# First tree's masks made by TensorE and ScalarE, three rows' statistics moved, experts' second product by halves, last tile stored in quarters

## The chip, the cores and the metric

The kernel runs on one core of one Trainium2 chip. A core has TensorE (PE in the profile, with its weight loads listed as PEld), VectorE (DVE), ScalarE (ACT), GpSimd (POOL) and SyncE (SP), which here only issues transfers. The metric is the device time of one execution in microseconds (us), as the median of several runs; lower is better.

## The reference

The input `x` is 4 rows of 512 tokens by 128 features. Six residual steps follow, each on the layer norm of `x`:

```python
x = x + 0.5 * fff_attention(ln(x))     # T: three trees q, k, v, then attention
x = x + attention(ln(x))               # h: 16 heads, rope, causal
x = x + 0.5 * fff_attention(ln(x))     # t
x = x + 0.5 * experts(ln(x))           # e: 8 experts, top 2, and a shared one
x = x + mamba(ln(x))                   # s: a scan over time, 16 states
x = x + 0.5 * experts(ln(x))           # f
```

A tree has 15 nodes and 16 leaves. Each token walks down four levels by the signs of the node scores and ends in one leaf; the output is that leaf's small network (128 to 64 to 128):

```python
sel = one_hot(leaf, 16)
hidden = relu(einsum('nd,ldh->lnh', x, w1) + b1) * sel.T[:, :, None]
out = einsum('lnh,lho->no', hidden, w2) + sel @ b2
```

An expert computes `(silu(x @ w1.T) * (x @ w3.T)) @ w2.T`, weighted by its gate.

## The kernel before

Everything is written as small generators, one for each row (0 to 3) and step, and `TIMES` gives each a planned start and end. The main loop always advances the job whose next step is planned earliest, so the code of many rows and steps is interleaved into one program text. From that text the framework makes the queue of each engine when the program is built: it may take an instruction ahead of older ones of the same engine if its inputs are expected to be ready. Waits between engines are semaphores, and each engine works through its own queue in order. SP's queue holds nearly all transfers, also in order.

**A tree step.** `tree_prep` computes the layer norm (`stats`: `bn_stats` at L290, `bn_aggr` at L292, an inverse root by tiny VectorE instructions from L300 to L283, the shift at L308; `layer_norm` at L316 or L318), turns it (`features`, L324 to L333), scores the nodes in three matmuls (`mm3`, L173 to L175: a product in two rounded parts), makes bits of the signs (L356) and multiplies by the leaf paths (L359). An entry of that product is zero where the token is in that leaf. `taken` (L361) is this as bytes for 48 leaves; it is written to memory (L363), and six transfers (L369) read it back, so that each leaf's row of 512 bytes lies on 64 partitions. That is `mask`, eight chunks of 128 hidden units by 512 tokens for each of the three trees, in two buffers. `sel` (L375) is the same selection in a float format for the bias product (L413).

`tree_main` then takes 24 chunks: `first` makes the hidden layer of a chunk (three matmuls into a PSUM bank of role `tree_mm`, or `start` for every other of the first eight) and applies bias and mask in one VectorE instruction, `full` (L400). `second` multiplies by the second weights into `tree_acc` (L410), five chunks later. For row 0 the weights come from the caller's arrays and are split into two parts by ScalarE and GpSimd or VectorE (`split_tree`, L161 and L162); they are also kept in memory for the other rows. `second_bias` folds a bias in (L234 to L240). Buffers of role `stage` (five) hold what is to be split, buffers of role `ring` (seven) hold weights. PSUM has eight banks; `tree_tr` is the role of the small products.

The calls 1 to 3 of `tree_prep` are those of rows 1, 3 and 2 in their first tree step. Each begins with `stats`, which reads only the loaded `x`, so the framework was free to put those instructions early.

**An expert step.** `expert_main` makes two hidden tiles for each expert (`u0`, `u1`, at L765 to L772) and multiplies them by the second weights in `second` (L780): for each of four 128-token tiles of the row, first the half with `u0`, then the half with `u1`, into one PSUM bank. ScalarE scales the result by the gate (L790) and GpSimd adds it to `x` (L791). The shared expert, which comes last, is added by VectorE in one instruction (L793). After the last step `store` writes the row out (L1013).

Of the kernel before, what the change touches and what calls it, by code (L numbers as in the profile page):

```python
# [15 lines left out]
F32 = mybir.dt.float32  # L16
F32R = mybir.dt.float32r
# [4 lines left out]
ALU = mybir.AluOpType  # L22
AX = mybir.AxisListType

P = 128
B, S, D = 4, 512, 128
NT = S // P
EPS = 1e-5

LEAVES, LEAF_W, DEPTH = 16, 64, 4  # L30
NODES = LEAVES - 1
NCH = LEAVES * LEAF_W // P
# [47 lines left out]
EXPERTS, INTER = 8, 256  # L80
# [32 lines left out]
def macaron(ctx: ExitStack, tc: tile.TileContext, t: dict, stages: int = 6):  # L113
    nc = tc.nc
# [6 lines left out]
    def bank(role):  # L121
        return psum.tile([P, S], F32, tag=role, name=role, bufs=BANKS[role])
# [4 lines left out]
    def tiny(shape, tag, bufs=2):  # L127

        n = int(np.prod(shape[1:]))
        if tag not in turns:  # L130
            first = taken_of[0]
            taken_of[0] += bufs * n
            assert taken_of[0] <= SCRATCH
            turns[tag] = cycle([scratch[:, first + n * i : first + n * i + n] for i in range(bufs)])
        out = next(turns[tag])
        if len(shape) == 2:
            return out
        names = "abcd"[: len(shape) - 1]
        sizes = dict(zip(names, shape[1:]))
        return out.rearrange(f"p ({' '.join(names)}) -> p {' '.join(names)}", **sizes)  # L140

    def work(role, shape=(S,), dtype=F32):

        return wp.tile([P, *shape], dtype, tag=role, name=role, bufs=BUFS[role])
# [11 lines left out]
    def flat(a):  # L156
        return a if len(a.shape) == 2 else a.rearrange("p a b -> p (a b)")
# [31 lines left out]
    x = [rows[:, b] for b in range(B)]  # L189
# [12 lines left out]
    leafpath, ident_h, future_t = (whole[:, ts(k, P)] for k in range(3))  # L202
    future = whole[:, 3 * P :]


    at = {}
    col = 0
# [59 lines left out]
    def inverse_root(out, v, s):  # L267

        shape = list(out.shape)
        y = tiny(shape, f"root_{shape[1]}", 4)  # L270
        nc.vector.tensor_scalar(
            y.bitcast(I32), v.bitcast(I32), -0.5, float(0x5F3759DF), ALU.mult, ALU.add
        )

        h = tiny(shape, f"square_{shape[1]}", 4)
        nc.vector.tensor_mul(s, y, v)
        nc.vector.tensor_mul(h, s, y)
        nc.vector.scalar_tensor_tensor(s, h, -10.0 / 3, h, ALU.add, ALU.mult)
        nc.vector.scalar_tensor_tensor(y, s, 5.0, y, ALU.add, ALU.mult)
        a = 0.375  # L280
        nc.vector.scalar_tensor_tensor(s, y, -0.5 * a**3, v, ALU.mult, ALU.mult)
        nc.vector.tensor_mul(s, s, y)
        nc.vector.scalar_tensor_tensor(out, s, 1.5 * a, y, ALU.add, ALU.mult)  # L283

    def stats(b, role, square=False):

        st = tiny([P, NT, 6], "bn", 4)
        mv = tiny([P, NT, 2], "mv", 4)
        for i in range(NT):
            nc.vector.bn_stats(st[:, i, :], x[b][:, i, :])  # L290
        for i in range(NT):
            nc.vector.bn_aggr(mv[:, i, :], st[:, i, :])  # L292
        n = 2 if square else 1
        rstd, shift = (tiny([P, n, NT], f"{r}_{n}", 4) for r in ("rstd", "shift"))

        ps = bank(role)
        var, step = (
            ps[:, k * n * NT : (k + 1) * n * NT].rearrange("p (n t) -> p n t", n=n) for k in range(2)
        )
        nc.vector.tensor_scalar_add(var[:, 0, :], mv[:, :, 1], EPS)  # L300
        if square:

            nc.vector.scalar_tensor_tensor(
                var[:, 1, :], var[:, 0, :], EPS, mv[:, :, 1], ALU.mult, ALU.add
            )
        inverse_root(rstd, var, step)
        mean = mv[:, :, 0].unsqueeze(1).to_broadcast([P, n, NT])
        nc.vector.scalar_tensor_tensor(shift, mean, -1.0, rstd, ALU.mult, ALU.mult)  # L308
        return [(rstd[:, k, :], shift[:, k, :]) for k in range(n)]

    def layer_norm(b, rstd, shift, on_act=False, role="ln"):
        ln = work(role)
        for i in range(NT):
            out, by, to = ln[:, ts(i, P)], rstd[:, i : i + 1], shift[:, i : i + 1]
            if on_act:
                nc.scalar.activation(out, x[b][:, i, :], AF.Identity, scale=by, bias=to)  # L316
            else:
                nc.gpsimd.tensor_scalar(out, x[b][:, i, :], by, to, ALU.mult, ALU.add)  # L318
        return ln
# [25 lines left out]
        return tuple(w), second_weights(k)  # L345

    def tree_prep(b, st):
        ln = layer_norm(b, *stats(b, "tree_tr")[0], st.call == 0)
        yield
        st.xn = xn = features(ln, "tree_tr")  # L350
        yield

        ps = bank("tree_tr")
        mm3(ps, nodes, xn)
        bits = work("bits", dtype=BF16)
        nc.vector.tensor_scalar(bits, ps, at["node_b"], 0.0, ALU.add, ALU.is_ge)  # L356
        yield
        ps = bank("tree_tr")
        nc.tensor.matmul(ps, lhsT=leafpath, rhs=bits, start=True, stop=True)  # L359
        taken = work("taken", dtype=U8)[:ALL_LEAVES]  # L360
        nc.vector.tensor_scalar(taken, ps[:ALL_LEAVES], 0.0, None, ALU.is_equal)  # L361
        rows = t["fff_taken"][st.call]
        nc.sync.dma_start(out=rows, in_=taken)  # L363
        st.masks = []
        for k in range(TREES):
            mask = work("mask", (NCH, S), U8)
            pairs = rows[k * LEAVES : (k + 1) * LEAVES].rearrange("(c l) s -> l c s", l=2)
            for m in range(2):
                nc.sync.dma_start(  # L369
                    out=mask[m * LEAF_W : (m + 1) * LEAF_W],  # L370
                    in_=pairs[m : m + 1].to_broadcast([LEAF_W, NCH, S]),
                )
            st.masks.append(mask)
        st.sel = work("sel", dtype=F32R)
        nc.vector.tensor_scalar(st.sel, ps, 0.0, None, ALU.is_equal)  # L375

    def tree_main(b, st):
        xn = st.xn
# [376 lines left out]
    def expert_main(b, st, last):  # L755
        xn = st.xn
        weights = [fetch_expert(e) for e in range(AHEAD)]

        def first(e, c):
            w13 = [weights[e][0][:, k, :] for k in range(2)]  # L760
            ps1, ps3 = bank("moe_1"), bank("moe_3")
            mm3(ps1, [m[:, ts(c, P)] for m in w13], xn)
            mm3(ps3, [m[:, ts(2 + c, P)] for m in w13], xn)
            u = work(f"u{c}")
            nc.scalar.activation(u, ps1, AF.Tanh, scale=0.5)  # L765
            nc.vector.scalar_tensor_tensor(u, u, 1.0, ps1, ALU.add, ALU.mult)  # L766
            if (2 * e + c) % POOL_E[0] < POOL_E[1]:
                v = work("v3")
                nc.scalar.copy(v, ps3)
                nc.gpsimd.tensor_mul(u, u, v)  # L770
            else:
                nc.vector.tensor_mul(u, u, ps3)  # L772
            return u

        def second(e, h):
            w2 = weights[e - e % 4][1]
            acc = bank("moe_acc")
            for i in range(NT):
                for c in range(2):
                    nc.tensor.matmul(  # L780
                        acc[:, ts(i, P)],
                        lhsT=h[c][:, ts(i, P)],
                        rhs=w2[:, e % 4 * 2 + c, :],
                        start=(c == 0),
                        stop=(c == 1),
                    )
            if e < EXPERTS:
                y = work("y")
                for i in range(NT):
                    nc.scalar.mul(y[:, ts(i, P)], acc[:, ts(i, P)], st.comb[:, i, e : e + 1])  # L790
                nc.gpsimd.tensor_add(flat(x[b]), flat(x[b]), y)  # L791
            else:
                nc.vector.scalar_tensor_tensor(  # L793
                    flat(x[b]), acc, 0.25, flat(x[b]), ALU.mult, ALU.add
                )

        later = Later(LAG_EXPERT)
        for e in range(EXPERTS + 1):
            if e + AHEAD < EXPERTS + 1:
                weights.append(fetch_expert(e + AHEAD))  # L800
            h = []
            for c in range(2):
                h.append(first(e, c))
                later.step()
                yield
            later.add(partial(second, e, h))
        while later.queue:
            later.step()
            if later.queue:
                yield  # L810
        if last:
            store(b)


# [370 lines left out]
def _constants():  # L1185

    f = np.float32
# [46 lines left out]
    for q in range(GROUPS):  # L1234
# [10 lines left out]
        "lower": np.broadcast_to(lower, (P, EXPERTS, EXPERTS)),  # L1245
        "state_w": np.concatenate([np.zeros((P, 6, P), f), gather.reshape(P, 1, P)], axis=1),
        "spread": spread.reshape(P, GROUPS * P),
    }, head


# [99 lines left out]
```

## Time and profile before

| What | Value |
|---|---|
| Median of the runs | 1130.06 us (1129.55 to 1131.53, three runs) |
| Profiled execution, its own time | 1134.71 us |
| Span of that execution | 1132.9 us |
| First product with masked values (L410) | begins 27.24 us after the start |
| First product of the k tree in row 0 | begins 34.18 us after the start |
| Last product of the last row | ends about 1128.3 us |
| Transfers of 512-byte mask rows (L369) | 48, 256 KB each |

The profiled execution is one run, 4.65 us slower than the median; of its 1134.71 us 1132.9 are the span in which the instructions of the profile lie. All times inside an execution are counted from the start of that span. Each line of a timeline is an engine, a line of the code, the operation, what it writes and reads, and the idle time ahead of it with what ended it.

### The profile page before, as it was taken

The page shows a single profiled execution, that of the slowest core. Times are in us where ns is not written, and L with a number is a line of the kernel's source. Part 1 is how long each engine was busy: PE and PEld are TensorE (multiplying, and loading weights), DVE is VectorE, ACT ScalarE, POOL GpSimd, SP SyncE. Part 2 cuts the span into 40 slices and gives each one's busy share as a digit, 9 for nine tenths or more (in the row PEclk, how much of TensorE's full clock was granted, in tenths as well). Part 3 has the DMA queues.
Part 4 walks back from the last instruction along what each step waited for, and adds up shares of the span by engine and source line. Part 5 has one row for each costly group of instructions (what it writes and reads, how often), then busy time and mean ns, then how long its engine had stood idle before and what let it go on. Part 6 is the DMA issues. An engine that isn't in the chain of part 4 may idle for free.

```text
span 1132.9 us, 16461 instructions
## 1 busy us (share of the span) xinstructions
PE 1065.0 (94%) x5536; PEld 717.4 (63%) x5536; DVE 903.5 (80%) x2151; ACT 516.4 (46%) x1078; POOL 408.3 (36%) x392
## 2 busy tenths in 40 slices
PE   3999999999999999999999999999598989997998
PEld 2666655566666767765566766567276646754787
DVE  4566886587576887775799997899989989999864
ACT  2231423332322555444443544465576557564544
POOL 2215231002100323220324651356626647666523
PEclk9999999999999999999999999999899989997999
DMA  7885845321542212243743334832137424742320
GB/s 217 261 254 168 284 109 119 84 69 57 123 124 93 65 37 69 87 112 115 208 137 139 117 94 107 277 130 107 38 117 254 133 66 146 249 121 70 113 88 10
DMA packets 79651, 146.41 MB, mean 129 GB/s; under 512 B 7536, under 2 KB 39664, under 8 KB 79568
## 3 DMA queue, kind: packets, MB, share of 16 engines
q1 hardware_dynamic: 79280, 145.07, 42.6%
q8 instruction: 44, 0.72, 0.3%
q14 instruction: 39, 0.32, 0.1%
q10 hardware_dynamic: 288, 0.30, 0.1%
HBM read 125.35 MB, written 13.70 MB: 123 GB/s over the span
## 4 chain that ended last, share of the span: by engine, by line
PE 61%; DVE 17%; issue 4%; ACT 4%; POOL 2%; DMA 1%; SPq 1%; POOLq 0%; ACTq 0%; DVEq 0%
PE tree_acc L410 9%; PE moe_acc L780 7%; DVE states L990 6%; PE head_acc L608 4%; PE head_sc L640 4%; PE moe L173 4%; PE head_max L564 4%; PE moe L175 3%; PE moe L174 3%; DVE states L989 3%; PE tree_mm L173 3%; PE tree_mm L175 3%; PE tree_mm L174 3%; PE state_acc L941 2%; DVE u L766 2%
## 5 line engine op out<-in xcount | busy, mean ns | idle before, releaser
L991 POOL TENSOR_TENSOR states<-states,cs 128x512 f32<-128x512 f32 x128 | 163.8, 1284 | 146.0 <-DVE states L990 87.8
L410 PE MATMUL tree_acc<-full,ring 128*128 128x512 f32 x384 | 193.4, 599 | 5.9 <-DVE full L400 4.9
L572 DVE CUSTOM_DVE_ANT_0 head_max<-head_max,kept 128x128 f32<-128x128 f32 (+3 forms) x256 | 126.8, 495 | 61.0 <-PE head_max L564 58.5
L400 DVE SCALAR_TENSOR_TENSOR full<-tree_mm,kept,mask 128x512 f32<-128x512 f32 x188 | 137.8, 746 | 42.4 <-PE tree_mm L175 37.7
L656 ACT ACTIVATE pt<-head_sc 128x512 f32<-128x512 f32 (+1 forms) x176 | 95.3, 559 | 139.2 <-PE head_sc L648 132.4
L780 PEld LDWEIGHTS moe_acc<-ring,u 128*128 128x128 f32 x1152 | 141.9, 195 | 21.2 <-DVE u L772 6.2
L990 DVE TENSOR_TENSOR_SCAN states<-decay,states 128x512 f32<-128x512 f32 x128 | 154.8, 1216 | 0.5 <-ACT decay L988 0.2
L780 PE MATMUL moe_acc<-ring,u 128*128 128x128 f32 x1152 | 146.4, 280 | 5.3 <-DVE u L772 3.1
L173 PE MATMUL moe<-xl,ring 128*128 128x512 f32 x288 | 129.1, 448 | 13.3 <-DVE u L766 4.7
L791 POOL TENSOR_TENSOR kept<-kept,y 128x512 f32<-128x512 f32 x64 | 83.0, 1298 | 142.2 <-ACT y L790 133.7
L988 ACT ACTIVATE decay<-dts,kept 128x512 f32<-128x512 f32 x128 | 88.5, 696 | 83.9 <-DVE states L990 67.0
L765 ACT ACTIVATE u<-moe 128x512 f32<-128x512 f32 x144 | 86.4, 601 | 72.2 <-PE moe L175 70.5
L174 PE MATMUL moe<-xh,ring 128*128 128x512 f32 x288 | 116.8, 405 | 0.0
L175 PE MATMUL moe<-xh,ring 128*128 128x512 f32 x288 | 115.7, 402 | 0.0
L766 DVE SCALAR_TENSOR_TENSOR u<-u,moe 128x512 f32<-128x512 f32 x144 | 97.4, 678 | 17.7 <-ACT u L765 15.2
L790 ACT ACTIVATE y<-moe_acc,scratch 128x128 f32<-128x128 f32 x256 | 73.3, 367 | 74.5 <-PE moe_acc L780 72.6
L548 POOL TENSOR_SCALAR km<-k_bias,kept 128x512 fp32r<-128x512 f32 x64 | 43.6, 699 | 157.2 <-PE head_sc L640 110.6
L173 PE MATMUL tree_mm<-xl,ring 128*128 128x512 f32 x188 | 98.1, 524 | 0.2 <-DVE states L990 0.2
L173 PEld LDWEIGHTS moe<-xl,ring 128*128 128x128 f32 x288 | 55.1, 191 | 63.5 <-DVE u L766 13.5
L410 PEld LDWEIGHTS tree_acc<-full,ring 128*128 128x128 f32 x384 | 70.8, 191 | 38.4 <-issue 19.9
L564 PE MATMUL head_max<-km,q_bias 120*128 120x512 f32 (+2 forms) x192 | 92.0, 479 | 1.1 <-ACT p L446 1.1
L989 DVE TENSOR_TENSOR states<-state_b,dtxs 128x512 f32<-128x512 f32 x128 | 85.9, 683 | 4.7 <-DMA dtxs<-state_rows 3.6
(257 smaller groups left out, 1946.1 us busy)
## 6 DMA issues: line engine op xcount, KB each, us to landing
ring<-moe_parts SPq DMA_DIRECT2D x72, 512.0 KB
ring<-tree_parts SPq DMA_DIRECT2D x42, 512.0 KB
ring<-in_fff_w SPq DMA_DIRECT2D x24, 512.0 KB
mask<-fff_taken SPq DMA_DIRECT2D x48, 256.0 KB
ring<-in_moe_w SPq DMA_DIRECT2D x16, 512.0 KB
dts<-state_rows SPq DMA_DIRECT2D x32, 256.0 KB
dtxs<-state_rows SPq DMA_DIRECT2D x32, 256.0 KB
moe_parts<-moe_w SPq DMA_DIRECT2D x9, 512.0 KB
```

Of the source, the lines that this page charges most:

```text
L173: nc.tensor.matmul(ps, lhsT=lh, rhs=rl, start=start, stop=False)
L174: nc.tensor.matmul(ps, lhsT=ll, rhs=rh, start=False, stop=False)
L175: nc.tensor.matmul(ps, lhsT=lh, rhs=rh, start=False, stop=stop)
L400: nc.vector.scalar_tensor_tensor(full, ps, neg_b1[:, n : n + 1], st.masks[k][:, c, :], ALU.max, ALU.mult)
L410: nc.tensor.matmul(acc, lhsT=weights[k][1][:, c, :], rhs=h, start=(c == 0), stop=False)
L564: nc.tensor.matmul(view, lhsT=qs[:R_MAX, g, ts(i, P)], rhs=km[j0 // 2][:R_MAX, j0 % 2 : j0 % 2 + each, :kw], start=True, stop=True,)
L572: nc.vector.tensor_tensor_reduce(view[:, n, :], view[:, n, :], future[:, S - kw :], -1.0, float(np.finfo(np.float32).max), ALU.add, ALU.mi ...
L766: nc.vector.scalar_tensor_tensor(u, u, 1.0, ps1, ALU.add, ALU.mult)
L780: nc.tensor.matmul(acc[:, ts(i, P)], lhsT=h[c][:, ts(i, P)], rhs=w2[:, e % 4 * 2 + c, :], start=(c == 0), stop=(c == 1),)
L989: nc.vector.tensor_mul(h, bs, dtx[g])
L990: nc.vector.tensor_tensor_scan(h, dA, h, 0.0, ALU.mult, ALU.add)
L991: last = nc.gpsimd.tensor_mul(h, h, cs[:, q])
```

## The change

There are four edits.

1. In the first call of `tree_prep` (row 0), the masks of the q tree no longer go through memory. A new constant `leaf_rows` (16 leaves by 8 chunks of 128, one where the hidden unit belongs to the leaf) is loaded on ScalarE's queue into a `stage` buffer and copied into a second one in the rounded format. `sel` is made ahead of `taken`. Then eight matmuls with 16 contraction rows spread `sel` over the 128 hidden units of each chunk, and eight ScalarE copies turn them into bytes. The k and v masks of row 0, and all masks of later calls, come by transfer as before.
2. In calls 1, 2 and 3 the first `bn_stats` may not be taken ahead of what VectorE was given before it in the program text.
3. `second` of the experts goes through all four tiles with `u0` and then through all four with `u1`; the flags that open and close the accumulation are set once for the bank.
4. For the shared expert of the last row in the last step, products keep the order by tile, the addition to `x` is made in four instructions, and each quarter is stored by a transfer of its own.

```diff
+    raw_rows, leaf_rows = (work("stage", [NCH * P], dt)[:LEAVES] for dt in (F32, F32R))
+    nc.scalar.dma_start(out=raw_rows, in_=t["leaf_rows"])
+    nc.scalar.copy(leaf_rows, raw_rows)
...
-            nc.vector.bn_stats(st[:, i, :], x[b][:, i, :])
+            first = nc.vector.bn_stats(st[:, i, :], x[b][:, i, :])
+            if late and i == 0:
+                tc.keep_in_program_order(first)
...
-        ln = layer_norm(b, *stats(b, "tree_tr")[0], st.call == 0)
+        ln = layer_norm(b, *stats(b, "tree_tr", late=0 < st.call < B)[0], st.call == 0)
...
+        st.sel = work("sel", dtype=F32R)
+        if st.call == 0:
+            nc.vector.tensor_scalar(st.sel, ps, 0.0, None, ALU.is_equal)
         taken = work("taken", dtype=U8)[:ALL_LEAVES]
...
+            st.masks.append(mask)
+            if st.call == 0 and k == 0:
+
+                for c in range(NCH):
+                    ps_c = bank("tree_tr")
+                    nc.tensor.matmul(
+                        ps_c, lhsT=leaf_rows[:, ts(c, P)], rhs=st.sel[:LEAVES], start=True, stop=True
+                    )
+                    nc.scalar.copy(mask[:, c, :], ps_c)
+                continue
...
-        st.sel = work("sel", dtype=F32R)
-        nc.vector.tensor_scalar(st.sel, ps, 0.0, None, ALU.is_equal)
+        if st.call:
+            nc.vector.tensor_scalar(st.sel, ps, 0.0, None, ALU.is_equal)
...
-            for i in range(NT):
-                for c in range(2):
...
+            at_end = last and b == B - 1 and e == EXPERTS
+            order = [(c, i) for c in range(2) for i in range(NT)]
+            for c, i in sorted(order, key=lambda ci: ci[::-1]) if at_end else order:
+                nc.tensor.matmul(
+                    acc[:, ts(i, P)],
+                    lhsT=h[c][:, ts(i, P)],
+                    rhs=w2[:, e % 4 * 2 + c, :],
+                    start=(c == 0 and (at_end or i == 0)),
+                    stop=(c == 1 and (at_end or i == NT - 1)),
+                )
...
-            else:
+            elif not at_end:
...
+            else:
+                for i in range(NT):
+                    out = x[b][:, i, :]
+                    nc.vector.scalar_tensor_tensor(out, acc[:, ts(i, P)], 0.25, out, ALU.mult, ALU.add)
+                    nc.sync.dma_start(out=t["out"][b, ts(i, P)], in_=out)
...
-        if last:
+        if last and b < B - 1:
             store(b)
...
+        "leaf_rows": np.kron(np.eye(LEAVES, dtype=f), np.ones((1, LEAF_W), f)),
```

More of the change, by code (lines that the diff above doesn't have):

```diff
@@ L283, in inverse_root, with stats @@
         nc.vector.scalar_tensor_tensor(out, s, 1.5 * a, y, ALU.add, ALU.mult)
-    def stats(b, role, square=False):
+    def stats(b, role, square=False, late=False):
         st = tiny([P, NT, 6], "bn", 4)
@@ L372, in tree_prep @@
                 )
-            st.masks.append(mask)
-        st.sel = work("sel", dtype=F32R)
-        nc.vector.tensor_scalar(st.sel, ps, 0.0, None, ALU.is_equal)
+        if st.call:
+            nc.vector.tensor_scalar(st.sel, ps, 0.0, None, ALU.is_equal)
     def tree_main(b, st):
@@ L777, in second @@
             acc = bank("moe_acc")
-            for i in range(NT):
-                for c in range(2):
[L780 to L786, printed above, removed]
+            at_end = last and b == B - 1 and e == EXPERTS
[8 more added lines that the diff above has]
+                )
             if e < EXPERTS:
```

## The prediction

> **What bounds the kernel now.** I read the page first: its busy table, its slices, its chain of work.
>
> ```profile
> PE 1065.0 (94%) x5536; PEld 717.4 (63%) x5536; DVE 903.5 (80%) x2151; ACT 516.4 (46%) x1078; POOL 408.3 (36%) x392
> ...
> PE   3999999999999999999999999999598989997998
> ...
> PE 61%; DVE 17%; issue 4%; ACT 4%; POOL 2%; DMA 1%; SPq 1%; POOLq 0%; ACTq 0%; DVEq 0%
> ```
>
> TensorE is busy in nearly every slice of 28 us. Only the first (3 tenths) and those from 800 us on, where VectorE's scan limits, have holes. In stretches of 5 us PE is at 5.00 nearly throughout from 30 to 580 us; so what is won ahead of 30 us should move all that follows, if the queues keep their order. The front is therefore read next, in order of time, VectorE and ScalarE first:
>
> ```profile
> 7.04 0.17 DVE L282 TENSOR_TENSOR tree_tr<-tree_tr,scratch 128x4 f32<-128x4 f32 x1
> ...
> 8.59 0.29 DVE L290 BATCH_NORM_STATS2 scratch<-kept 128x6 f32<-128x128 f32 x1 [1.38 <-DMA kept<-in_x]
> 8.80 0.14 DVE L283 SCALAR_TENSOR_TENSOR scratch<-tree_tr,scratch 128x4 f32<-128x4 f32 x1
> 8.86 1.22 DVE L162 TENSOR_TENSOR ring<-stage,ring 128x1024 fp32r<-128x1024 f32 x1
> 9.99 0.15 DVE L308 SCALAR_TENSOR_TENSOR scratch<-scratch 128x4 f32<-128x4 f32 x1
> ...
> 10.18 1.65 ACT L316 ACTIVATE ln<-kept,scratch 128x128 f32<-128x128 f32 x4 [1.40 <-DMA ring<-in_fff_w]
> ```
>
> Row 0's last step of the root (L283) stands behind row 1's first statistics, which wait 1.38 us for row 1's `x`; then a weight split comes between it and L308, and the layer norm starts at 10.18. The same timeline further on:
>
> ```profile
> 17.55 0.68 DVE L361 TENSOR_SCALAR taken<-tree_tr 48x512 uint8<-48x512 f32 x1 [1.36 <-PE tree_tr L359]
> ...
> 19.94 1.37 SPq L369 DMA_DIRECT2D mask<-fff_taken  x2
> ...
> 21.41 0.57 SPq L166 DMA_DIRECT2D stage<-in_fff_w  x1
> ...
> 26.44 0.75 DVE L400 SCALAR_TENSOR_TENSOR full<-tree_mm,kept,mask 128x512 f32<-128x512 f32 x1 [2.94 <-DMA mask<-fff_taken]
> ...
> 27.24 2.08 PE L410 MATMUL tree_acc<-full,ring 128*128 128x512 f32 x2 [4.92 <-DVE full L400]
> ...
> 28.78 1.05 ACT L161 CAST ring<-stage 128x1024 fp32r<-128x1024 f32 x1 [5.80 <-DMA stage<-in_fff_w]
> ```
>
> The selection is known at 18.2, but the q masks land at 26.4; PE has filled its banks and stands 4.92 us. In 27.24 to 30.39 the table by stretches grants PE a clock of 0.50. The k weights, issued behind the masks on SP, land at 28.8. And the end:
>
> ```profile
> 1128.99 0.69 DVE L793 SCALAR_TENSOR_TENSOR kept<-moe_acc,kept 128x512 f32<-128x512 f32 x1 [2.60 <-POOL kept L791]
> 1129.71 0.39 SPq L1013 DMA_DIRECT2D out<-kept  x1
> ```
>
> The last addition waits for GpSimd's addition of the expert before (ends 1128.96), not for PE (done at 1128.3).
>
> **The parts, and their cost.** Savings are minus.
>
> (a) *Row 0's layer norm.* Without row 1's statistics ahead of it, L283 can follow L282 at 7.24 and L308 at 7.45. ScalarE then decides: its weight cast runs 7.74 to 8.78, so the layer norm starts at 8.8 behind it (-1.4) or at 7.6 ahead of it (-2.6); if the split still stands before L308, at 10.2 (0). The load of `leaf_rows` (64 KB, some 0.2 us at the 280 to 370 GB/s of 3 to 9 us) may delay that cast by 0.2. Its issue (0.45, as the two ScalarE issues before it) and its copy of 1024 columns (1.05, as the cast of 1024 columns at L161) fall in ScalarE's idle 1.37 and 2.55 us ahead of 4.96 and 7.74; without that cover the copy would cost its 1.05. I take -1.4 + 0.2 = -1.2, the order that the queue has now; bounds -2.6 to +1.3 (0 + 0.2 + 1.05).
>
> (b) *PE's stall for the masks.* After (a), `sel` is ready at 17.55 - 1.2 + 0.7 = 17.05 (now first, at `taken`'s place). One matmul (0.4) and one ScalarE copy of 512 columns (0.58, the row of L332) later the first chunk is there at about 18.1, and `full` can run 8 us sooner. ScalarE is idle from 15.7 to 22.7 (6.98 us before L239), enough for 8 x 0.58 = 4.6. Six banks hold waiting chunks, so the copies may have only one or two of the eight; with one, a chunk takes matmul, copy and two handovers, about 1.2, still under the 1.55 us in which PE does a chunk (period of 36.66 and 38.21). So the 4.92 go, and the slow clock with them: 27.24 to 30.39 held 3.15 us of what takes 1.55 later, 1.6. Sum -6.5; bounds -6.5 to -4.9.
>
> (c) *Eight more matmuls on PE*, 512 columns each: 0.23 start to start where PE runs at its later pace, 0.42 in the first 17 us. +1.8; bounds +1.8 to +3.4.
>
> (d) *Is the k tree ready?* In the trace its weights are whole at 32.3 (cast 28.78, GpSimd's part to 32.3) and PE comes to them at 34.18; it would now come at 34.18 - 1.2 - 6.5 + 1.8 = 28.3. Two mask issues (1.37) leave SP ahead of the load, and `taken` comes 1.2 - 0.7 = 0.5 earlier, so it is issued near 19.5. If it takes the 7.4 us it took (21.41 to 28.78, beside 512 KB of mask rows that are now gone), then 1.05 and 2.38, it is whole at 30.4: +2.1. If it moves like the last store (0.5 us until data flow, 256 KB from 1130.6 to 1131.8), 512 KB land 3.3 after issue, the weights are whole at 26.3, and it costs nothing. If it comes no sooner at all, +4.0. The first mask rows were what it shared the transfers with, so I lean to the short end: +0.5. The k masks, issued behind it, are needed at about 29.5 and have 9 us where they had 13.
>
> (e) *Statistics moved.* Row 1's took 0.85 + 0.37 + about 2.0 us of VectorE that was idle; rows 2 and 3 had 1.2 us each early, and their tiny steps already came later. Row 1's now stand behind its tenth chunk, near 30; its layer norm comes near 35, and its transposes, at 45.74 before, are wanted near 39.5: 4 us of slack. VectorE is busy 2.0 to 3.4 of 5 us from 35 to 65, so PE's three chunk banks bridge it. Rows 2 and 3 fall in 95 to 130, where VectorE has 2.8 to 4.8 of 5. +0.3; bounds 0 to +2.4 (all of the two rows' instructions in PE's way).
>
> (f) *Experts' products by halves.* The work is the same. PE waits for the second half where the first could run, 0.97 us of matmuls. The view of waits:
>
> ```profile
> PE moe_acc L780 <- DVE u L772: 3.1, 6, 0.7
> ```
>
> 3.1 us in six waits is the most to win, and some of it lies where the scan limits. -1.0; bounds -3.1 to 0.
>
> (g) *End by quarters.* The additions still start at 1128.99. The first quarter (0.35, row of L468) is issued at 1129.4, and four issues of 0.39 end at 1130.9, 0.8 later than the one did. The one transfer moved data from 1130.6 to 1131.8, of which a quarter needs 0.3 instead of 1.2. So +0.8 - 0.9 = -0.1; bounds -0.5 to +0.8. The Trainium skill, in DMA: Bandwidth & Descriptors (Rules for kernel authors), advises to merge small transfers, since under 64 KB most of the time is overhead; by the section Anatomy of one DMA, with about 2.0 us fixed each, the last of four would land at 1132.9, which speaks against this part and would make it +1.1 instead of -0.1 against the 1131.8 of the trace.
>
> Sum: -1.2 - 6.5 + 1.8 + 0.5 + 0.3 - 1.0 - 0.1 = **-6.2 us**. The profiled execution's 1134.71 would be 1128.5 (span 1126.7); the median 1130.06 becomes **1123.9**.
>
> **The rivals.**
>
> *A, the transfers hide it.* From 22 to 48 us the transfers' mean share is about 1.0, and the k weights come no sooner than 32.3. Then PE only gains its 1.9 us of lateness there: -1.9 + 0.3 - 1.0 - 0.1, 1127.4. For it: that share. Against it: from 17 to 22 the share is 0.0 to 0.4, and in 30 to 130 PE waits for no transfer.
>
> *B, a new wait in ScalarE's queue: slower.* The cast of the k weights stands ahead of some mask copies in ScalarE's queue. All behind it then waits until the weights land. If they land at 25.0, copies resume at 26.05 and `full` at 26.7 (0.3 later than in the trace), and the eight matmuls come on top: +2.1. If they land at 28.8 as now, it is +4.0 + 1.8. Midway, +4.0, with (e), (f) and (g) at -0.8: +3.2, 1133.2. It decides if the cast precedes the copies and the weights land after 23. For it: ScalarE waited 5.80 us on this load already. Against it: the copies can run from 17.5 on, long before.
>
> *C, another order later.* Queues are not in the order of the code (row 1's statistics stood ahead of row 0's), so new times at the front may reorder what follows. From 780 to 1060 us PE is idle for 36 us; a fifth more costs 7: 1131, between 1126 and 1135. Nothing in the profile says which way it goes.
>
> **How the numbers follow.** Forecast 0.62, A 0.14, C 0.14, B 0.10. The forecast's own range is 1119.2 (all at the far bound: -2.6 - 6.5 + 1.8 - 3.1 - 0.5 = -10.9) to 1127.6 (weights late by 2.1, statistics at 2.4: +1.6 + 2.1 on the sum). With A inside and most of B and half of C left out, 1118.5 to 1131.0 leaves under 2 in 10 outside. A measurement of this kernel tells about 0.2% (2.3 us) from no change. Faster: 0.62 x 0.97 + A 0.08 + C 0.02 = 0.70. Same: 0.13. Slower: B 0.10 and half of C, 0.17.
>
> **What would show it.** (a) holds if `ln` L316 starts by 9.0. (b): first `full` near 18, no idle of microseconds before L410, clock 1.00 through 27 to 31. (c): eight matmuls at about 0.23. (d): k tree's first matmul near 28, cast of its weights by 24. (e): `bn_stats` of row 1 near 30, no wait for VectorE after it. (f): the wait on L772 ahead of L780 gone. (g): last issue near 1130.9 less the gain. The prediction is wrong if the first `full` comes early and the k tree still starts after 32 (A), if copies wait behind a cast (B), or if the state steps' idle grows (C).

## The result and the profile after

| | before | after |
|---|---|---|
| median of 5 runs each, same chip | 1130.19 us (1129.55 to 1131.73) | 1142.14 us (1137.98 to 1145.73) |
| ratio, with its 95% interval | 1 | 1.0101 (1.0084 to 1.0119) |
| profiled execution, span | 1134.71, 1132.9 | 1137.98, 1136.2 |

The change makes the kernel 12.0 us slower; 6.2 us faster was forecast. The page of the changed kernel:

```profile
PE 1068.1 (94%) x5544; PEld 714.7 (63%) x5544; DVE 905.7 (80%) x2154; ACT 523.8 (46%) x1087; POOL 409.0 (36%) x392
...
PE   5999999999999999999999999999699989986998
...
PEclk9999989999999999999999999999899999998999
...
PE 62%; DVE 19%; issue 4%; POOL 3%; ACT 2%; DMA 1%; SPq 0%; POOLq 0%; DVEq 0%; ACTq 0%
```

TensorE has its eight matmuls more, the first slice is fuller, and the chain of work that ended last is led by TensorE as it was. New is the 8 in the sixth slice of the clock, 142 to 170 us, where the kernel before had a 9. The front, in the timelines of TensorE, VectorE and ScalarE (start, duration, then what ended the idle time before):

```profile
9.34 1.65 ACT L322 ACTIVATE ln<-kept,scratch 128x128 f32<-128x128 f32 x4 [2.75 <-DVE scratch L314]
11.34 1.04 ACT L161 CAST ring<-stage 128x1024 fp32r<-128x1024 f32 x1 [0.36 <-DMA stage<-in_fff_w]
...
14.30 0.79 PE L173 MATMUL tree_tr<-xl,rounded 128*128 128x512 f32 x1 [2.79 <-ACT q_bias L509]
...
18.57 0.69 DVE L368 TENSOR_SCALAR sel<-tree_tr 128x512 fp32r<-128x512 f32 x1 [1.78 <-PE tree_tr L365]
...
20.76 0.75 DVE L418 SCALAR_TENSOR_TENSOR full<-tree_mm,kept,mask 128x512 f32<-128x512 f32 x1 [0.91 <-ACT mask L384]
...
22.08 0.59 ACT L384 CAST mask<-tree_tr 128x512 uint8<-128x512 f32 x1 [0.27 <-PE tree_tr L381]
...
22.40 0.50 PE L381 MATMUL tree_tr<-sel,stage 16*128 16x512 f32 x1
22.83 0.50 PE L173 MATMUL tree_mm<-xl,ring 128*128 128x512 f32 x1
23.26 0.49 PE L381 MATMUL tree_tr<-sel,stage 16*128 16x512 f32 x1
...
25.83 1.06 ACT L161 CAST ring<-stage 128x1024 fp32r<-128x1024 f32 x1
...
27.58 1.02 PE L428 MATMUL tree_acc<-full,ring 128*128 128x512 f32 x2
...
31.14 0.80 PE L173 MATMUL tree_mm<-xl,ring 128*128 128x512 f32 x1
```

The first mask is used at 20.76 instead of 26.44 and TensorE has no stall before L428. But its matmuls start every 0.43 us from 20 to 24, and the k tree's first product (31.14) comes 3.0 us earlier than before with two pairs of second products (L428) fewer done ahead of it, so that only 1.2 us are won.

To see where the rest went, instructions of one line and engine were matched in order between two traces, and the median shift taken over a stretch. Against the profiled execution of before the changed kernel stands at -1.2 us from 60 to 78, at 0.0 from 95 to 120, and at +9.1 from 185 to 800. Single executions differ at the front too: with edit 3 or edit 4 alone, which leave the front as it was, this shift is +1.4 and +0.6 from 60 to 78, so -1.2 is no more than what such executions differ by. Behind 800 us the profiled execution of before is itself a long one (the last section has the numbers), and the shift falls to +2.5; so the two spans differ by 3.3 us where the medians differ by 12.0. The 9 us are lost in one place. It is the tree whose selection was made at 143.4 us. Its four statistics ran at the very front (in the run with edit 2 for row 2 alone, further on, this group is one short). In the timelines of before:

```profile
10.93 0.85 DVE L290 BATCH_NORM_STATS2 scratch<-kept 128x6 f32<-128x128 f32 x4
...
123.45 0.21 DVE L300 TENSOR_SCALAR tree_tr<-scratch 128x4 f32<-128x4 f32 x1
...
134.99 0.14 DVE L308 SCALAR_TENSOR_TENSOR scratch<-scratch 128x4 f32<-128x4 f32 x1
...
135.25 1.73 POOL L318 TENSOR_SCALAR ln<-kept,scratch 128x128 f32<-128x128 f32 x4 [5.80 <-DVE scratch L308]
...
143.38 0.68 DVE L361 TENSOR_SCALAR taken<-tree_tr 48x512 uint8<-48x512 f32 x1 [1.00 <-PE tree_tr L359]
```

and after:

```profile
145.82 0.29 DVE L294 BATCH_NORM_STATS2 scratch<-kept 128x6 f32<-128x128 f32 x1
...
146.35 0.17 DVE L306 TENSOR_SCALAR tree_tr<-scratch 128x4 f32<-128x4 f32 x1
...
150.16 0.16 DVE L314 SCALAR_TENSOR_TENSOR scratch<-scratch 128x4 f32<-128x4 f32 x1
...
150.44 3.44 POOL L324 TENSOR_SCALAR ln<-kept,scratch 128x128 f32<-128x128 f32 x8 [3.13 <-DVE scratch L314]
...
150.93 1.76 PE L330 MATMUL tree_tr<-kept,ln 128*128 128x128 f32 x4 [1.15 <-POOL ln L324]
...
158.63 0.68 DVE L370 TENSOR_SCALAR taken<-tree_tr 48x512 uint8<-48x512 f32 x1 [1.83 <-PE tree_tr L365]
```

The chain of the inverse root began at 123.45 and could take eleven microseconds between other work. Now the first of its four statistics runs at 145.82 and the root needs all four, so the root starts 22.9 us later, and the selection is made 15.3 us later. What TensorE does meanwhile stands in the table by stretches of 1 us (busy time of PE, PEld, DVE, ACT and POOL, with instructions in brackets; then the granted clock):

```profile
149.00:150.00 1.00, 0.78 (x5) 0.46 (x5) 0.94 (x9) 0.00 (x0) 0.00 (x0) 1.00 0.08 16
150.00:151.00 1.00, 0.07 (x1) 0.07 (x1) 0.90 (x6) 0.00 (x0) 0.56 (x2) 1.00 0.00 0
151.00:152.00 1.00, 0.80 (x3) 0.34 (x3) 0.11 (x2) 0.00 (x0) 1.00 (x3) 1.00 0.09 25
152.00:153.00 1.00, 0.90 (x4) 0.58 (x3) 0.00 (x0) 0.27 (x1) 1.00 (x3) 0.50 0.00 0
...
157.00:158.00 1.00, 1.00 (x4) 0.39 (x3) 0.00 (x0) 0.00 (x0) 0.00 (x0) 0.50 0.09 16
```

Two of these stretches in the kernel before:

```profile
150.00:151.00 1.00, 1.00 (x16) 0.58 (x14) 0.87 (x4) 0.54 (x1) 1.00 (x2) 1.00 1.01 211
...
157.00:158.00 1.00, 1.00 (x6) 0.85 (x5) 0.83 (x3) 0.00 (x0) 0.00 (x0) 1.00 0.00 0
```

TensorE runs out of work at 150 (busy 0.07), and then its clock is 0.50 from 152 to 158.8. From 148 to 160 it starts 32 matmuls; in the kernel before it starts 59.

### The profile page after: what moved, and what is told of

Read it like the earlier page. It is cut to its first block, busy times and chain, and to the rows that moved or that the text cites. A ratio compares the mean times of both kernels' runs of the same rounds, so it can differ in the third digit from the quotient of the medians.

```text
span 1136.2 us, 16491 instructions
## 1 busy us (share of the span) xinstructions
PE 1068.1 (94%) x5544; PEld 714.7 (63%) x5544; DVE 905.7 (80%) x2154; ACT 523.8 (46%) x1087; POOL 409.0 (36%) x392
## 4 chain that ended last, share of the span: by engine, by line
PE 62%; DVE 19%; issue 4%; POOL 3%; ACT 2%; DMA 1%; SPq 0%; POOLq 0%; DVEq 0%; ACTq 0%
PE tree_acc L428 10%; PE moe_acc L801 6%; DVE states L1016 6%; PE head_acc L626 5%; PE head_sc L658 4%; PE head_max L582 4%; PE moe L173 3%; DVE states L1015 3%; PE tree_mm L173 3%; PE moe L175 3%; PE moe L174 3%; PE tree_mm L174 3%; PE tree_mm L175 3%; DVE u L784 2%; DVE u L790 2%
## 5 line engine op out<-in xcount | busy, mean ns | idle before, releaser
L428 PE MATMUL tree_acc<-full,ring 128*128 128x512 f32 x384 | 192.9, 596 | 0.9 <-DVE full L418 0.9
L801 PEld LDWEIGHTS moe_acc<-ring,u 128*128 128x128 f32 x1152 | 139.2, 191 | 18.7 <-DVE u L790 3.2
L801 PE MATMUL moe_acc<-ring,u 128*128 128x128 f32 x1152 | 143.7, 277 | 4.8 <-DVE xb L907 1.7
L428 PEld LDWEIGHTS tree_acc<-full,ring 128*128 128x128 f32 x384 | 70.5, 189 | 32.1 <-issue 18.0
```

The costliest lines, as they stand in the source:

```text
L428: nc.tensor.matmul(acc, lhsT=weights[k][1][:, c, :], rhs=h, start=(c == 0), stop=False)
L801: nc.tensor.matmul(acc[:, ts(i, P)], lhsT=h[c][:, ts(i, P)], rhs=w2[:, e % 4 * 2 + c, :], start=(c == 0 and (at_end or i == 0)), stop=(c = ...
```

## The experiments

The first four runs take the change apart. The kernel before, beside these runs: 1130.57 us (21 runs). Edits are named by their numbers in the section on the change.

**All but edit 2** (the changed kernel with its statistics free again):

```diff
-        ln = layer_norm(b, *stats(b, "tree_tr", late=0 < st.call < B)[0], st.call == 0)
+        ln = layer_norm(b, *stats(b, "tree_tr", late=False)[0], st.call == 0)
```

> The changed kernel with the statistics of rows 1 to 3 free again; the other three edits stay. Theory P (the row 3 statistics, held in program order, come some 15 us later than TensorE needs that row's first products; it runs dry near 148 us and loses 9): about 1133, and row 3's first transposes come at their old place near 136 instead of 150.9. Rival M (the new way of making masks disturbs the order of what follows, whatever the statistics do): stays at 1139 or more. Rival H (the products by halves cost): stays at 1139 or more.

Measured: 1135.04 us, ratio 1.0043 (1.0028 to 1.0059). **Edit 2 alone**, the kernel before with the diff's `late` lines:

```diff
+            if late and i == 0:
+                tc.keep_in_program_order(first)
```

> The kernel before with the statistics' edit alone. Theory P: 1138 to 1141, with TensorE idle and its clock at half near 150 us. Rivals M and H: within 2 us of 1130.2, since neither masks nor halves are in it.

Measured: 1138.83 us, 1.0073 (1.0060 to 1.0086); shift +0.1 until 120, +9.0 from 185. So edit 2 costs 8.3 us by itself, with the loss at the place shown, and some 4.5 are left without it. **Edit 1 alone**, with `leaf_rows`, the eight products and their copies as in the diff:

```diff
+                    nc.tensor.matmul(
+                        ps_c, lhsT=leaf_rows[:, ts(c, P)], rhs=st.sel[:LEAVES], start=True, stop=True
+                    )
+                    nc.scalar.copy(mask[:, c, :], ps_c)
```

> The kernel before with the masks' edit alone. Theory P: 1127 to 1130, the front wins about 1 to 2 us and keeps it. Rival M: 1138 or more.

Measured: 1136.82 us, 1.0054 (1.0035 to 1.0073). A miss for the theory that this edit gains, and less than rival M's 1138: it is the second loss. **Edit 3 alone**, with its flags as in the diff:

```diff
+            for c, i in sorted(order, key=lambda ci: ci[::-1]) if at_end else order:
```

> The kernel before with the experts' products by halves alone. Theory P: 1127 to 1131, the waits on the second half (3.1 us in all) are the most it can win. Rival H: 1135 or more.

Measured: 1131.33 us, 1.0007 (0.9995 to 1.0019), no difference that can be told.

The next two, and the first two variants of edit 1 further on, stand beside 1131.16 us (34 runs) of before. **Edit 4 alone:**

```diff
+                for i in range(NT):
+                    out = x[b][:, i, :]
+                    nc.vector.scalar_tensor_tensor(out, acc[:, ts(i, P)], 0.25, out, ALU.mult, ALU.add)
+                    nc.sync.dma_start(out=t["out"][b, ts(i, P)], in_=out)
```

> The kernel before with the last row's end tile by tile alone; nothing else is moved. Forecast (term g): 1130 to 1131, within 0.1% of before. If the small stores cost more than the hidden subtraction saves: 1131 to 1132. In the trace the last four additions and stores should stand one behind the other in the last 3 us and everything ahead of them at before's times.

Measured: 1132.19 us, 1.0002 (0.9992 to 1.0012), no difference that can be told. **Edit 2 for the third call only** (row 3's first tree):

```diff
-        ln = layer_norm(b, *stats(b, "tree_tr")[0], st.call == 0)
+        ln = layer_norm(b, *stats(b, "tree_tr", late=st.call == 2)[0], st.call == 0)
```

> The kernel before with the late statistics for row 3's tree alone (the third tree), not for rows 1 and 2 of it. Theory P (row 3's whole norm now starts at 146 us, behind its first statistic, TensorE runs out at 148 and is then clocked down): all of the cost is here, 1138 to 1141. Rival: the pins of the other two rows carry a part: 1133 to 1136.

Measured: 1132.84 us, 1.0017 (1.0007 to 1.0026). The theory had the wrong tree: the one of 135 us did not move in this run, and row 3's first statistic went to 167 us, where it costs about 3 us in the profiled execution (shift -0.7 at 165, +2.7 from 178). So the same edit was tried for the other two calls, `late=st.call == 3` (row 2) and `late=st.call == 1` (row 1), beside 1129.49 us (19 runs) of before:

> The kernel before with the late statistics for row 2's first tree alone (the fourth call). The run with row 3's pin cost 1.7 us and left the tree of 135 us untouched, so that tree must be row 2's. Theory P2 (this tree's whole chain waits for its first statistic, 11 us later than before; TensorE runs out at 148 us): most of the 8.3 us of the three pins, 1136 to 1139. Rival (the three pins together, not this one): under 1134.

> The kernel before with the late statistics for row 1's first tree alone (the second call); the queues of the other engines stay as before. Prediction (e): row 1's chain comes near 37 us, 4 us of slack are enough, 1130 to 1131.5. Rival: its tree is late for TensorE too, 1133 or more.

Measured: **row 2's 1140.79 us, 1.0095 (1.0078 to 1.0111); row 1's 1129.46 us, 0.9995 (0.9984 to 1.0006)**. The timelines of the run with row 2's alone repeat the changed kernel's:

```profile
145.69 0.29 DVE L291 BATCH_NORM_STATS2 scratch<-kept 128x6 f32<-128x128 f32 x1
...
150.31 3.44 POOL L321 TENSOR_SCALAR ln<-kept,scratch 128x128 f32<-128x128 f32 x8 [4.34 <-DVE scratch L311]
...
150.81 1.61 PE L327 MATMUL tree_tr<-kept,ln 128*128 128x128 f32 x4 [1.16 <-POOL ln L321]
```

This one instruction is the first cause. The single prices (11.3, 1.7 and 0.0) do not add up to the 8.3 of the three together. Up to 800 us the profiled executions agree better: row 2's alone is 7.5 us behind at 185 to 300 us, all three together 8.7 to 9.0. So some 4 of the 11.3 lie behind 800 us, where executions differ anyway (last section). Row 3's late statistic finds a schedule that is already late: in the changed kernel it runs at 174.46 and its tree's transposes at 181.01, before at 172.32, which is no more than the 9 us that everything is late there.

**Why does the masks edit lose?** Three variants of edit 1 with the leaf rows in a buffer of their own:

```diff
-    raw_rows, leaf_rows = (work("stage", [NCH * P], dt)[:LEAVES] for dt in (F32, F32R))
+    raw_rows = work("stage", [NCH * P])[:LEAVES]
+    leaf_rows = const.tile([LEAVES, NCH * P], F32R, tag="leaf_rows", name="leaf_rows")
```

> Masks by TensorE alone, as in the run of that name, but the 16 rows stand in a buffer of their own, so that they hold no place among the buffers that the weights' loads pass through (there the first weight's load was issued at 4.5 us rather than 1.8). Theory M1 (the late weights took the gain of the front): the weight's load is back at 1.8 us, the first accumulation comes before 27 us, and the time is 1126 to 1130. Theory M2 (the gain is lost between 80 and 165 us, where the new order on VectorE's queue puts row 2's norm behind waits for TensorE): the front gains but the shift against before climbs by 3 to 4 us between 80 and 165 us, 1132 to 1137.

Measured: 1134.18 us, 1.0033 (1.0021 to 1.0045). The first weights' load, issued at 4.74 us in the changed kernel, is back at 1.8 us; the shift is -0.8 at 60 to 78, +1.7 at 95 to 120 and +2.7 from 170. The same, with the copies on two engines:

```diff
-                    nc.scalar.copy(mask[:, c, :], ps_c)
+                    (nc.vector.tensor_copy if c % 2 else nc.scalar.copy)(mask[:, c, :], ps_c)
```

> As the run before it, with every second of the eight mask copies on VectorE rather than ScalarE. If the copies' pace (0.85 us a mask on ScalarE) holds up TensorE's first chunks: TensorE ends the first chunks 2 to 3 us earlier than there and the time is 2 us lower. If it does not (M2): the same time within 1 us.

Measured: 1135.36 us, 1.0035 (1.0020 to 1.0051). The front gains 1.7 us more than in the run before it (-2.5 at 60 to 78). Of these, 0.8 were there already when the first of the eight products started (19.09 beside 19.86); the other 0.9 came while they ran, so the copies' pace did hold up TensorE. By 180 us the shift is +2.6 all the same. The same as the first of the three, with products in the banks `start`:

```diff
-                    ps_c = bank("tree_tr")
+                    ps_c = bank("start")
```

> Masks by TensorE alone, leaf rows in a buffer of their own, and the eight products in banks of the role start rather than tree_tr; built so, the queues behind the front stand nearly as in the kernel before. Theory M2: the front's gain (1 to 2 us) is kept, no climb between 80 and 180 us, 1127.5 to 1130. Rival (the masks' own work): 1132 to 1136 as the other two.

Measured beside 1129.49 us (19 runs): 1139.23 us, 1.0089 (1.0064 to 1.0114). Here the front itself was 2.4 us longer: the products and the chunks took turns in the same banks, and from 21 to 31 us the granted clock was 0.50. So this run does not tell the theories apart for the front, but it shows how 1.0 us is lost later. In the timelines of GpSimd and TensorE:

```profile
88.18 1.28 POOL L162 TENSOR_TENSOR moe_w<-stage,moe_w 128x512 fp32r<-128x512 f32 x1 [4.48 <-ACT moe_w L161]
89.58 1.73 POOL L325 TENSOR_SCALAR ln<-kept,scratch 128x128 f32<-128x128 f32 x4
...
90.08 1.62 PE L331 MATMUL head_tr<-kept,ln 128*128 128x128 f32 x4 [0.44 <-POOL ln L325]
```

An expert weight whose load came late is split just ahead of the layer norm of row 0's head, and TensorE waits for that norm; before, the split was done by 83.1 and the norm started at 86.14. The split holds up VectorE too: the last step that the norm needs, L315, starts at 88.33 and takes 1.15 us, to the end of the split; in the kernel before (L308 at 85.87) it took 0.16. The experts themselves are planned for after 270. The last variant has all eight copies on VectorE (`nc.vector.tensor_copy(mask[:, c, :], ps_c)`, banks `tree_tr`):

> Masks by TensorE, leaf rows in a buffer of their own, products in the banks tree_tr and all eight copies on VectorE; of the mask kernels built this is the one whose later queues differ least from those of before (VectorE's in a few places, ScalarE's in the place of two expert weights). Theory M2: the front's gain (1 to 2.5 us at 60 us) is mostly kept behind 180 us, 0.997 to 1.000. Rival (the masks' own work, or any mask kernel): the shift climbs by 3 us or more between 80 and 180 us, 1.003 or more.

Measured beside 1130.59 us (17 runs): 1135.28 us, 1.0040 (1.0026 to 1.0055). The gain of the front is kept longest here: -1.5 at 60 to 120. It is gone by 146 (+0.3), and the ratio says 4.5 us longer; that cannot all come from the stretch up to 180. It is a miss for theory M2, which wanted the gain kept.

**The load alone.** The kernel before with edit 1's load and copy, and nothing made of them, first in two `stage` buffers, then with a buffer of its own as above:

```diff
+    raw_rows, leaf_rows = (work("stage", [NCH * P], dt)[:LEAVES] for dt in (F32, F32R))
+    nc.scalar.dma_start(out=raw_rows, in_=t["leaf_rows"])
+    nc.scalar.copy(leaf_rows, raw_rows)
```

> The kernel before with the load and the copy of the 16 leaf rows into two stage buffers, as the changed kernel has them, and nothing made of them: no matmul, no mask copy, masks by transfer as before. The work of TensorE is that of before. Theory M2 (what the masks edit loses behind 80 us is another order of the queues, not its work): the order changes as much as with the masks, and the shift against before climbs by 2 to 4 us between 80 and 180 us; 1132 to 1136. Rival (the loss is the masks' own work): 1130 to 1131.5.

> As the run with the load and copy of the leaf rows alone, but into a buffer of its own, so that the stage buffers turn as in the kernel before; the queues then stand almost as in the kernel before. Theory M2 (the load cost 3.7 us there by the other order alone): the same as before, 0.999 to 1.001. Rival (the transfer of 64 KB and the copy at the front cost it): 1.003 as there.

Measured: 1133.21 us beside 1129.49, **1.0034 (1.0022 to 1.0046)**; with its own buffer 1133.45 beside 1130.59, **1.0018 (1.0008 to 1.0028)**. The first gives TensorE no work, yet its shift, +0.7 at 60 to 78, climbs to +1.7 at 100 and +4.2 at 160. One of the steps, in the timelines of VectorE and TensorE:

```profile
98.29 0.69 DVE L528 SCALAR_TENSOR_TENSOR head_k<-rot,head_k 128x512 fp32r<-128x512 f32 x1 [2.11 <-ACT head_k L527]
98.89 1.41 DVE L406 SCALAR_TENSOR_TENSOR full<-tree_mm,kept,mask 128x512 f32<-128x512 f32 x2
...
100.35 0.50 PE L173 MATMUL tree_mm<-xl,ring 128*128 128x512 f32 x1 [1.29 <-DVE full L406]
```

Two chunks wait behind a head's product on VectorE, and TensorE for their banks. VectorE's part alone is no difference: in the kernel before it does the same, the head's product at 98.20 and then

```profile
98.81 1.40 DVE L400 SCALAR_TENSOR_TENSOR full<-tree_mm,kept,mask 128x512 f32<-128x512 f32 x2
```

but there TensorE starts its next chunk at 98.81 and waits for nothing. Why it had a bank there and none here was not traced. In the second run the shift is -0.2 to +0.2 until 800, as theory M2 wants; but M2's 1.000 is missed by 1.8 parts in a thousand, which must come later. By their ratios the two runs cannot be told apart, their intervals overlap; what tells them apart is the shift of one execution each. In the last 250 us its queues differ from those of before in a few places: on ScalarE two scalings of expert results stand earlier and `decay` steps one place later, on SP some `state_rows` stores and expert weights change places.

**The changed kernel again**, unchanged, twice, one execution each beside 1129.21 us of before:

> The changed kernel once more with a profile, since its first profiled execution (1137.98) was the shortest of five and the median (1142.14) is 4 us longer. Theory D (the rest lies in the last 250 us, where TensorE idles behind the scan and its clock is lowered in steps of 1.1 to 1.5 us each, in some executions oftener than in others): up to 800 us as in the first profile within 0.5 us, then two or three such steps more if the time is near 1142. Rival: the extra lies in the front or at 145 us, where the starved stretch could be longer.

> As the run before it, a third execution of the changed kernel with a profile: the same two theories, the same numbers.

Measured: 1138.46 and 1142.87 us. The first of them lost 1.3 us less at the starved stretch than the execution profiled at first; its clock was 0.50 for 3.4 us there, not for 6.8. The second is longer than the first profiled execution by 2.0 us up to 120 us (its front comes 1.4 later) and by 3.0 at one place; the table by stretches of 20 us shows it, first in the changed kernel's first execution:

```profile
920.00:940.00 20.00, 16.79 (x79) 9.93 (x80) 19.81 (x36) 12.39 (x28) 8.12 (x7) 1.00 0.25 81
```

then in the third:

```profile
920.00:940.00 20.00, 17.28 (x73) 10.70 (x73) 17.09 (x28) 10.33 (x21) 7.16 (x6) 0.83 0.25 81
```

So theory D holds for 3 of these 5 us, and not for the 2 at the front.

## Why the prediction was wrong

**(e), the statistics: the step that failed.** It priced VectorE's time for them (+0.3, at most +2.4), let those of rows 2 and 3 "fall in 95 to 130", and counted on their tiny steps, which "already came later", to be behind them still. In the changed kernel row 2's first statistic ran at 145.82 and row 3's at 174.46. Row 2's tiny steps stood at 123.45 to 134.99 in the trace of before, so they had to move too. What the edit moves is not 1.2 us of work but the start of a chain that ends in TensorE's next tree: 22.9 us later at its head, 15.3 at its selection. The three together cost 8.3 us without the other edits, row 2's instruction alone 11.3, of which 7.5 up to 800 us. The prediction should have asked where the program text has that instruction, and what TensorE does behind it. For row 1 the step was right: its first statistic came at 34.67 in the changed kernel, near the 30 that it gave, and alone it cost nothing.

**(a) to (d), the front: -5.4 forecast, -1.2 found** (-0.6 and +0.2 in the two later executions). (a) The layer norm started at 9.34, not 8.8, and the weights' cast moved behind it and ahead of the features, so the node scores came 0.54 us later (14.30 to 13.76) instead of 1.2 earlier; the load of these weights was issued at 4.74, before at 1.79. (b) Right in kind: no stall before L428 and no lowered clock from 27 to 31. The lowered clock is not gone from every kernel with the masks: in the run of all but edit 2 it was 0.50 from 24.2 to 27.6. (c) The mis-sized term. Eight products were to cost 0.23 each. They share three banks with copies that take 0.59 and a handover of 0.27, and TensorE's queue has them in turn with the chunks: 16 matmuls from 19.61 to 25.57 took 5.96 us, at 0.23 they take 3.7. So +1.8 became about +4.1, beyond its bound of +3.4. The run with two copying engines, 0.9 us better while the products ran, bears this pace out. (d) The weights were cast at 25.83, not by 24, and did not hold up anything: 0 for +0.5. In sum +0.5 - 6.5 + 4.1 = -1.9, against -1.2 found; the 0.7 between them is less than what executions with an unchanged front differ by.

**Rival C was undervalued, and looked in the wrong place.** It had 0.14 and 1131, and put the cost into TensorE's idle time from 780 to 1060 us; that is 37.1 us in the changed kernel beside 36.0. The order changed earlier. Every kernel with the masks has other queues behind the front, and each lost 1.7 us or more between 78 and 180 us: -2.5 became +2.7, -1.5 became +0.2. That another order alone can cost it, with no mask in the kernel, is what the load in the `stage` buffers (+4.2 at 160) beside the load in its own (-0.2) speaks for, by one execution each; of the single steps only the one at 88 us was followed to its cause. So the first loss, edit 2's, is shown by experiment, and why edit 1 loses is in part argued. What was not shown: what the later queues cost behind 800 us. The two kernels whose shift is still 0 to +0.3 at 800 are 2.0 and 4.5 us longer by their ratios; that the few moved instructions there are the cause was not tried alone.

**(f)** -1.0 forecast, within the bounds: the wait it counted on, 3.1 us in six, has

```profile
PE moe_acc L801 <- DVE u L790: 1.5, 4, 0.7
```

in the changed kernel's view of waits, so about half of it went. The time does not show it: by its interval edit 3 alone changes it by -0.6 to +2.1 us, which holds the bound of 0 but not the -1.0. **(g)** -0.1 forecast with a top bound of +0.8. In the changed kernel

```profile
1131.48 0.89 DVE L820 SCALAR_TENSOR_TENSOR kept<-moe_acc,kept 128x128 f32<-128x128 f32 x4 [2.60 <-POOL kept L812]
1131.80 1.76 SPq L821 DMA_DIRECT2D out<-kept  x4
```

the span ends 4.7 us after the first addition starts, before 3.9; in the run with edit 4 alone it is 4.3. So it cost 0.4 to 0.8; other executions with the old end took 3.8 to 4.4, so the size is rough. The four issues lie 0.44 apart, 0.39 reckoned; what was too good was the landing of the last quarter: the span ends 2.6 us after its issue, before 2.8 us after that of the whole, where 0.9 less was counted on. The estimate from the Trainium skill, DMA: Bandwidth & Descriptors (Anatomy of one DMA), +1.1, had the sign right where the sum's -0.1 had it wrong, and was too high; that section is about transfers issued by GpSimd, and these are issued by SP.

In all: edit 2 takes some 7 to 8 us, edit 1 some 4 to 6, edits 3 and 4 nothing that can be told. The three profiled executions of the changed kernel are 9.1, 7.3 and 10.6 us behind by 800 us; the other 3 or so of the 12.0 lie behind that and are traced to no edit. None of the fourteen variants is faster than the kernel before by more than the measurement can tell.

## What to carry to other kernels

An instruction of 0.3 us that is moved has to be priced by the chain that starts with it: find its last consumer on the engine that sets the time, and the slack there. In a kernel whose queues are made anew at each build, a change at the front is also a change of everything behind it; build the suspected side effect alone (here a load that nobody uses) before crediting or blaming the work itself. A buffer that a new constant holds in a shared rotation can be part of its price.

## What the runs showed of the hardware

TensorE's clock was halved after a stretch without any long gap: from 148 to 152 its records leave 1.75 of 4 us idle, in gaps of 1.15 us and less, and the granted clock was 0.50 from 152.0 to 158.8. In the two later executions of the changed kernel it was 0.50 for 3.4 and 6.8 us there. The Trainium skill, TensorE: Matmul & The Clock Gate (Part 1: The HAM clock gate), gives an idle window of about 3.4 us as what lowers the clock. Read as a gap of that length, it would have lowered nothing here; the rows decide. How much idle time it takes the runs do not say: in the kernel before, a gap of 1.62 us at 813 left the clock at 1.00, and in the run with row 3's statistic alone the longest gap in the 3.4 us ahead of a lowering at 177.6 was 0.69 us.

Such lowerings last 3.4 us or two, three or four times that in the middle of all 18 kept traces, and behind 780 us they come and go between executions of the same kernel: one of 3.4 us at 1088 made 1.5 us between two executions, the one of 6.8 us at 921 made 2.9 of the 4.9 us above. They go with most of the spread there. The stretch from 800 us (moved by the shift) to the end of the span takes 326.7 to 328.3 us in the seven traces where the clock is lowered for 17 to 21 us between 780 and 1110, and 328.6 to 332.9 in the eleven where it is 24 to 34. The profiled execution of before has the most, 34 us and 332.9; the first of the changed kernel 20 and 327.1.

GpSimd can stretch a tiny VectorE instruction. The 18 kept traces have 4176 VectorE instructions on 128x4 numbers, as in the steps of the inverse root. Of these, 4108 take at most 0.34 us (0.16 in the median) and 68 take 0.38 to 1.29 us, and every one of the 68 ends within 0.04 us of the end of a GpSimd instruction, as in the split at 88 us above.
